# Masked attention on one core: how finished tokens are turned back and added to x, and which engine squares the queries

## The chip, the core and the metric

The kernel runs on one core of one Trainium2 chip. The core has TensorE (PE, matrix multiplies; its weight loads are shown apart as PEld), VectorE (DVE), ScalarE (ACT), GpSimd (POOL) and SyncE (SP), which only starts transfers (DMAs) here. Each engine works through its own queue in order. The metric is the time of one execution in microseconds (us), as the median of several runs.

## The reference

x has 8 batches of 512 features and 1,024 tokens, and the mask has one 0 or 1 for each token of a batch. There are 8 heads of 64 features; queries, keys and values are the same projection.

```python
xt = jnp.transpose(x, (0, 2, 1))
q = xt @ Wq.T
qh = q.reshape(B, T, NH, dk).transpose(0, 2, 1, 3)
scores = scale * jnp.einsum('bhqd,bhkd->bhqk', qh, qh)
logits = (scores * cmask + (1.0 - cmask) * NEG) * rmask
attn = jax.nn.softmax(logits, axis=-1)
ctx = jnp.einsum('bhqk,bhkd->bhqd', attn, qh)
out = ctx.transpose(0, 2, 1, 3).reshape(B, T, D) @ Wo.T
return x + jnp.transpose(out, (0, 2, 1))
```

A masked token attends evenly to all tokens, so every masked token of a batch has the same result, and no token attends to a masked key except those.

## The kernel before

About half of the tokens of a batch are kept by the mask. The kernel gathers them (at most 575, in 5 chunks of 128, the last of 64), puts the mean of x in the last place for all masked tokens, runs attention on these 576 tokens alone, and spreads the results back over the 1,024 tokens. (A second function, `attention_of_all_tokens`, does the same without gathering, and runs only where a mask keeps too many tokens or a sum gets too small; it doesn't run here.)

The work is a sequence of 32 pairs (b, pr): batch b from 0 to 7 and, in each, pr from 0 to 3, two heads of 64 features at a time. The document calls the stretch of a pair a stage. The order of all instructions is written by hand: the loop in `late` (L1067) goes through the pairs, and in each through five chunks c of keys. In a chunk stand `scores` (TensorE: 8 matmuls into `s`; ScalarE: two exps into `e`, L616), `add_up` of the chunk before (VectorE: the sums of `e`, L633), and tasks for other pairs that `tasks_of` (L884) lists with a cost and that are spread over the chunks by these costs; at the end of the pair comes `attend` (L657: TensorE, 40 matmuls into `av`, copied to `cT` by ScalarE). `s` has two buffers.

What the steps touch:

- Queries: `project` (L534) for the pair two places ahead, then `values` (L554): TensorE turns the queries into `v`, ScalarE copies it out (L565), VectorE squares it (`sq`, L570), sums the squares (`len`, L572) and takes the maximum (`top`, L579). `bias_of` (L581) turns `top` into the exps' bias, a pair later.
- End of a pair: `add_up(before, LAST)` and `invert(before)` (L713) in chunk 0 of the next pair: VectorE makes inverses `ri`, turns them (`rt`, L719), SP stores them and loads them back as `rb`. `contexts(before)` (L742) multiplies `cT` by `rb` on VectorE, in chunk 2, 3, 3 or 4 for pr = 0, 1, 2, 3.
- Next x: `turn` (L430), four times a batch, in pr=0 chunks 0, 2, 4 and pr=1 chunk 1: VectorE turns 128x1024 elements in 32x32 blocks (`xt`, L444), writing the four features of a row side by side, and SP stores `xt` to DRAM (`xd`, L452), four transfers of 32 rows. `search` (VectorE) finds which rows are kept, and `gather` (GpSimd, `xin`, L507) fetches them at the end of pr=1. `collect` (L515) turns `xin` into `xc` on TensorE at the beginning of pr=2.
- Output of batch b-1: `output` (L752) in pr=0 (two chunks), pr=1 (two) and pr=2 (one): TensorE multiplies the four `cT` of the batch by Wo into `po`, the fourth of them the `cT` of the pair just before, when the batch has just begun. ScalarE copies `po` to `oc`, GpSimd stores it to DRAM (`od`).
- Back to all tokens: `load_rest` (L809) loads x of batch b-1 again in pr=1 chunk 2 (`xr`, eight tiles of 128x512). `fetch` (L830) in pr=3 gathers, for each of eight groups of 128 tokens, the rows of `od` that these tokens own (`g`, L833; `origin` says which). `finish` (L841), eight tasks in pr=3: TensorE turns four 128x128 squares of `g` into `o` (L845), VectorE adds `o` from PSUM to `xr` (L848), and SP stores `xr` to the output (L850). `issue_stores` (L876) sends a store one chunk after its task.
- The last two batches end otherwise: batch 6 is finished by `finish` after the last pair, batch 7 by `finish_tokens`.

The tiles that pass through PSUM take turns in four banks (`bank`), besides the four that `s` takes.

Of the kernel before, what the change touches and what calls it, by code (L numbers as in the profile page):

```python
# [21 lines left out]
Q = 32  # L22
# [296 lines left out]
def attention_of_kept_tokens(ctx, tc, x, mask, wq, wo, out, ident, wqT, woT, verdict, flag):  # L319
# [49 lines left out]
    key = keep.tile([P, NC], F32, name="key")  # L369
    kept = keep.tile([P, B], F32, name="kept")  # L370
    origin = keep.tile([P, B, NT], I32, name="origin")
    pads = keep.tile([P, B, NC], F32, name="pads")
    pens = keep.tile([P, B, NC], F32, name="pens")
    low = keep.tile([P, 2, LAST], F32, name="low")
# [179 lines left out]
    def values(pair):  # L554
        nm = "%d_%d" % pair
        qT = qTs[pair]
        v = sb.tile([P, NC, P], F32, tag="v", name=f"v_{nm}", bufs=4)
        for at, n in ((0, LAST), (LAST, 1)):
            pt = bank(f"v_{nm}_{at}")
            for i in range(n):  # L560
                c = at + i
                nc.tensor.transpose(  # L562
                    pt[:, i * P : (i + 1) * P], qT[:, c * P : (c + 1) * P], ident
                )
            nc.scalar.copy(  # L565
                v[:, at : at + n, :], pt[:, : n * P].rearrange("p (c d) -> p c d", d=P)
            )
        vs[pair] = v
        sq = sb.tile([P, NC, P], F32, tag="sq", name=f"sq_{nm}", bufs=1)
        nc.vector.tensor_tensor(sq, v, v, ALU.mult)  # L570
        lengths = sb.tile([P, 2 * NC], F32, tag="len", name=f"len_{nm}")
        nc.vector.tensor_reduce(  # L572
            lengths,
            sq.rearrange("p c (h d) -> p (c h) d", h=2),
            axis=AX.X,
            op=ALU.add,
        )
        tops[pair] = sb.tile([P, 1], F32, tag="top", name=f"top_{nm}")
        nc.vector.tensor_reduce(tops[pair], lengths, axis=AX.X, op=ALU.max)  # L579
# [213 lines left out]
    def end_output(b, i):  # L793
# [12 lines left out]
        nc.vector.tensor_tensor(oc[:n, :], po[:n, :], partials[i][:n, :], ALU.add)  # L806
        nc.sync.dma_start(ods[b][places[i], :], oc[:n, :])

    def load_rest(b):  # L809
        for r in range(NN):  # L810
            for d in range(ND):
                xr = sb.tile([P, NB], F32, tag="xr", name=f"xr_{b}_{r}_{d}", bufs=NN * ND)
                nc.sync.dma_start(xr, x[b, d * P : (d + 1) * P, r * NB : (r + 1) * NB])
                xrs[b, r, d] = xr

    def fetch_last(b):

# [12 lines left out]
    def fetch(b):  # L830
        for i in range(NT):
            g = sb.tile([P, D], F32, tag="g", name=f"g_{b}_{i}", bufs=NT)
            nc.gpsimd.indirect_dma_start(  # L833
                out=g,
                out_offset=None,
                in_=ods[b],
                in_offset=bass.IndirectOffsetOnAxis(ap=origin[:, b, i : i + 1], axis=0),
            )
            gs[b, i] = g

# [43 lines left out]
    def tasks_of(p):  # L884

        b, pr = pairs[p]
        front, back, end = [], [], []
        if p + 2 < len(pairs):
            ahead = pairs[p + 2]
            front = [(2.0, lambda hf=hf: project(ahead, hf)) for hf in range(2)]  # L890
            front.append((0.6, lambda: values(ahead)))
            if p == 0:
                behind = pairs[1]
                front = [
                    (2.0, lambda: project(behind, 1)),
                    (0.6, lambda: values(behind)),
                    front[0],
                    (0.3, lambda: bias_of(behind)),
                    *front[1:],
                ]  # L900
        if p == ND - 1:
            back = [(0.5, lambda d=d: turn_weights(woT, "wo", d)) for d in range(ND)]
        if b + 1 < B and pr == 2:
            front = [(0.5, lambda i=i: collect(b + 1, i)) for i in range(NC)] + front
        if b > 0:
            if pr < 3:
                mine = {0: (0, 1), 1: (2, 3), 2: (4,)}[pr]
                (back if pr else end).extend((3.6, lambda i=i: output(b - 1, i)) for i in mine)
            elif b + 1 < B:
                t = 0.5  # L910
                back += [(t, lambda r=r, d=d: finish(b - 1, r, d)) for r in range(NN) for d in range(ND)]
        if p + 1 == len(pairs):
            end = [(2.7, lambda i=i: begin_output(b, i)) for i in range(NC)]
        return mix(front, back) + end
# [29 lines left out]
    def early():  # L944
# [98 lines left out]
        mean_first()  # L1043
        pt = bank("home_t")
        nc.tensor.transpose(pt[:, :BC], home, ident[:BC, :BC])
        nc.vector.tensor_copy(origin, pt[:, :BC].rearrange("p (b c) -> p b c", c=NT))

    def late():
        weights["wq"] = load_weights(wq, "wq")
# [14 lines left out]
        bias_of(pairs[0])  # L1064

        TURN = [(0, 0), (0, 2), (0, 4), (1, 1)]
        for p, pair in enumerate(pairs):  # L1067
            b, pr = pair
            before = pairs[p - 1] if p else None
# [3 lines left out]
            for c in range(NC):  # L1073
                scores(pair, c)
                if c:
                    add_up(pair, c - 1)
                if c == 0 and before:
                    add_up(before, LAST)
                    if p + 1 < len(pairs):
                        invert(before)  # L1080
                    else:
                        inv = inverses(before)
                if p + 1 == len(pairs):
                    if c == 1:
                        spread(before, inv)
                        contexts(before)
                elif c == (2, 3, 3, 4)[pr] and before:
                    contexts(before)
                if 0 < p < len(pairs) - 1 and c == 1:
                    bias_of(pairs[p + 1])  # L1090
                if b + 1 < B:
                    if (pr, c) in TURN:
                        turn(b + 1, TURN.index((pr, c)))
                    if pr < 2 and pr * NC + c < NN * ND:
                        add_features(b + 1, pr * NC + c)
                    if pr == 1 and c == LAST:
                        mean_of(b + 1)
                    if pr == 1:
                        search(b + 1, c)
                    if pr == 0 and c == 1:  # L1100
                        queries_of(b + 1)
                    if pr == 1 and c == LAST:
                        for i in range(NC):
                            gather(b + 1, i)
                if pr == 2 and c == 0 and b + 2 < B:
                    load_batch(b + 2)
                    load_ranks(b + 2)
                if pr == 1 and c == 2 and b > 0:
                    load_rest(b - 1)
                if pr == 3 and c == 0 and b > 0:  # L1110
                    fetch(b - 1)
                while todo and (c or p + 1 < len(pairs)) and (done < share * (c + 1) - 0.3 or c == LAST):
                    cost, task = todo.pop(0)
                    task()
                    done += cost
                issue_stores()
# [125 lines left out]
```

## Time and profile before

| what | value |
|---|---|
| median of 3 runs | 776.83 us (776.33 to 778.43) |
| the profiled execution | 778.43 us, of which its span from first to last instruction is 776.2 us |
| mean granted TensorE clock over the span | 0.966 |
| TensorE busy | 710.6 us |
| VectorE busy | 546.8 us |
| ScalarE busy | 356.6 us |
| DMA traffic | 119.53 MB, 154 GB/s |
| one batch in the middle (four stages) | some 90 us |

A busy time is the time in which an engine had an instruction in work, over the whole span. A wait in the profile names the instruction that stood, what released it, the total, the number of times and the longest. A group of instructions has its line, engine, operation, tiles and shapes, its count, the busy time, the mean duration of one in nanoseconds, and the idle time of the engine just before them. A timeline row has its start and its duration; rows of VectorE may overlap by some 0.08 us, so that steps from start to start are a little shorter than durations. In a row of windows stand the stretch, its length, the busy time of PE, PEld, DVE, ACT and POOL, the granted clock, the share of DMA time and the GB/s.

### The profile page before, as it was taken

To read this page: it belongs to the slowest core of one execution; us is meant where nothing else is said; L and a number is where in the kernel's file an instruction comes from. 1 tells how busy PE (TensorE), PEld (TensorE's weight loads), DVE (VectorE), ACT (ScalarE), POOL (GpSimd) and SP (SyncE) were. 2 spreads that over 40 slices of the span, in tenths; PEclk is the share of its full clock that TensorE was granted. 3 is DMA by queue.
4 is the path that set the end of the run, shared out by engine and by line. 5 is a ranking of instruction groups with operands and counts; after the bars stand their busy time and mean duration, and the time that the engine had idled before them with its cause. 6 is when DMAs were issued, how large, how long until landed. Compare 5 with 4: busy or idle time off the path is not lost.

```text
span 776.2 us, 12232 instructions
## 1 busy us (share of the span) xinstructions
PE 710.6 (92%) x4187; PEld 407.8 (53%) x4187; DVE 546.8 (70%) x1517; ACT 356.6 (46%) x727; POOL 168.9 (22%) x208
## 2 busy tenths in 40 slices
PE   6699898999989998999989999899989999898984
PEld 5555564556544564446635565445645566454443
DVE  6189878676867778586976768777785867556353
ACT  3366465454534544545444545345454444345300
POOL 4712010043102510034100521025100340004021
PEclk9799999999989999999989999999999999999996
DMA  7543503477235752377243773367532742146138
GB/s 272 164 144 112 175 19 91 119 239 258 99 93 164 217 217 79 106 212 268 100 128 105 221 253 127 99 193 222 177 107 79 226 136 90 64 153 204 38 126 266
DMA packets 86713, 119.53 MB, mean 154 GB/s; under 512 B 15744, under 2 KB 48576, under 8 KB 86640
## 3 DMA queue, kind: packets, MB, share of 16 engines
q1 hardware_dynamic: 69888, 76.27, 31.5%
q0 software_dynamic: 12528, 40.28, 15.9%
q10 hardware_dynamic: 4224, 2.10, 0.9%
q8 instruction: 35, 0.57, 0.3%
q14 instruction: 38, 0.31, 0.1%
HBM read 75.41 MB, written 43.19 MB: 153 GB/s over the span
## 4 chain that ended last, share of the span: by engine, by line
PE 69%; DVE 11%; DMA 6%; ACT 5%; issue 4%; SPq 1%; POOL 1%; POOLq 0%; DVEq 0%; ACTq 0%
PE s L612 17%; PE av L649 16%; PE pq L543 15%; PE po L762 10%; DMA xin<-xd,source 4%; ACT e L616 3%; PE o L845 3%; PE xc L522 3%; DVE junk L633 2%; DVE xt L444 2%; PE pa L782 2%; PE v L562 1%; ACT v L565 1%; DVE len L572 1%; DMA xr<-in_x_dram 1%
## 5 line engine op out<-in xcount | busy, mean ns | idle before, releaser
L633 DVE CUSTOM_DVE_ANT_0 junk<-e,valid 128x576 f32<-128x576 f32 x256 | 193.4, 756 | 77.9 <-ACT e L616 73.1
L612 PE MATMUL s<-qT 64*128 64x288 f32 (+1 forms) x1280 | 190.3, 442 | 7.8 <-ACT e L616 6.9
L616 ACT ACTIVATE e<-s,bias 128x576 f32<-128x576 f32 x256 | 176.6, 742 | 33.9 <-PE s L612 27.3
L612 PEld LDWEIGHTS s<-qT 64*128 64x128 f32 (+1 forms) x1280 | 95.1, 179 | 98.0 <-issue 57.5
L762 PE MATMUL po<-woT,cT 128*128 128x512 f32 (+1 forms) x336 | 124.4, 551 | 20.2 <-DVE cT L745 20.2
L543 PE MATMUL pq<-xc,wqT 128*128 128x288 f32 x512 | 138.1, 415 | 0.0
L649 PE MATMUL av<-e,v 128*64 128x288 f32 x1024 | 132.4, 409 | 0.9 <-DVE m L587 0.2
L543 PEld LDWEIGHTS pq<-xc,wqT 128*128 128x128 f32 x512 | 92.7, 190 | 36.3 <-issue 9.6
L649 PEld LDWEIGHTS av<-e,v 128*64 128x64 f32 x1024 | 71.1, 137 | 53.5 <-issue 7.0
L771 POOL DMA_DIRECT2D od<-oc x42 | 23.9, 570 | 331.1 <-ACT oc L769 312.4
L762 PEld LDWEIGHTS po<-woT,cT 128*128 128x128 f32 (+1 forms) x336 | 49.3, 178 | 78.4 <-issue 48.3
L665 ACT COPY cT<-av 128x288 f32<-128x288 f32 x62 | 22.4, 401 | 143.5 <-PE av L649 86.7
L833 POOL DMA_INDIRECT g<-od,origin x56 | 61.0, 1089 | 38.9 <-issue 17.2
L769 ACT COPY oc<-po 128x512 f32<-128x512 f32 (+1 forms) x35 | 19.1, 547 | 97.0 <-PE po L762 97.0
L444 DVE STREAM_TRANSPOSE xt<-x 128x1024 f32<-128x1024 f32 x28 | 57.7, 2062 | 0.0
L550 ACT COPY qT<-pq 128x288 f32<-128x288 f32 x64 | 25.5, 399 | 65.8 <-PE pq L543 61.5
L507 POOL DMA_INDIRECT xin<-xd,source x40 | 40.4, 1010 | 48.0 <-DVE sums L633 30.4
L570 DVE TENSOR_TENSOR sq<-v 128x640 f32<-128x640 f32 x32 | 26.3, 820 | 27.3 <-ACT v L565 22.8
L495 DVE TENSOR_SCALAR_CACHE_REDUCE junk<-rank,key 128x1024 f32<-128x1024 f32 (+4 forms) x40 | 39.9, 998 | 1.0 <-ACT rank L1015 0.8
L848 DVE TENSOR_TENSOR xr<-o,xr 128x512 f32<-128x512 f32 x56 | 36.3, 683 | 5.2 <-PE o L845 3.4
L587 DVE TENSOR_REDUCE m<-top 128x1 f32<-128x128 f32 x32 | 9.3, 289 | 41.2 <-PE top L585 41.0
L633 DVE CUSTOM_DVE_ANT_0 junk<-el,part 128x288 f32<-128x288 f32 x64 | 29.1, 454 | 12.1 <-ACT el L616 10.9
(133 smaller groups left out, 656.3 us busy)
## 6 DMA issues: line engine op xcount, KB each, us to landing
xr<-in_x_dram SPq DMA_DIRECT2D x64, 256.0 KB
x<-in_x_dram SPq DMA_DIRECT2D x56, 256.0 KB
xd<-xt SPq DMA_DIRECT2D x112, 128.0 KB
out_dram<-xr SPq DMA_DIRECT2D x56, 256.0 KB
rb<-row SPq DMA_DIRECT2D x60, 160.0 KB
od<-oc POOLq DMA_DIRECT2D x28, 256.0 KB
rank<-ranks SPq DMA_DIRECT2D x6, 512.0 KB
xd<-xt POOLq DMA_DIRECT2D x8, 256.0 KB
```

The lines of the kernel that those rows point to most:

```text
L444: nc.vector.transpose(xt.rearrange("p k (f d) -> p k d f", d=ND), xs[b][r][:, :, at : at + n].rearrange("p d (k t) -> p k d t", t=Q),)
L495: nc.vector.tensor_scalar(junk[:, :n], rank[:, i * P :], key[:, col], 0.0, ALU.is_le, ALU.add, accum_out=found[:, col])
L507: nc.gpsimd.indirect_dma_start(out=xin[:n, :], out_offset=None, in_=xds[b], in_offset=bass.IndirectOffsetOnAxis(ap=searches[b][2][:n, i : ...
L543: nc.tensor.matmul(pq[:, :KH], wqT[:, d, pr * P : (pr + 1) * P], xcs[b][:, d, cols], start=(d == 0), stop=(d == ND - 1),)
L570: nc.vector.tensor_tensor(sq, v, v, ALU.mult)
L612: nc.tensor.matmul(s[to, h, :KH], qT[heads[h], keys], qT[heads[h], queries], start=True, stop=True)
L616: nc.scalar.activation(e[:, hf if c < LAST else 0, :, :], s[:, :, :KH], AF.Exp, bias=biases[pair][:, c : c + 1], scale=SCALE,)
L633: nc.vector.tensor_tensor_reduce(junk[:, :n].rearrange("p (f k) -> p f k", k=KH), e[:, :, h, :], (valid if c < LAST else part).rearrange(" ...
L649: nc.tensor.matmul(av[head, :KH], v[keys, c, head], e[keys, hf if c < LAST else 0, h, :], start=(c == 0), stop=(c == LAST),)
L762: nc.tensor.matmul(po[k * n : (k + 1) * n, :w], cTs[b, pr][:, i * P : i * P + n], woT[:, pr, k * w : (k + 1) * w], start=(pr == 0), stop=( ...
L833: nc.gpsimd.indirect_dma_start(out=g, out_offset=None, in_=ods[b], in_offset=bass.IndirectOffsetOnAxis(ap=origin[:, b, i : i + 1], axis=0),)
L848: nc.vector.tensor_tensor(xr, pt, xr, ALU.add)
```

## The change

For batches 0 to 5 (`BLOCKS`), TensorE's transposes of `finish` are replaced by VectorE's 32x32 blocks. `block_origin` deals the tokens to `g` in another order, so that after a transpose of each 32x32 block the partitions hold 32 features and a quarter of the tokens: quadrant a (32 partitions) holds tokens 256 a to 256 a + 255, features on its 32 partitions and in 16 steps along the row. `place_blocks` makes `block_origin` by 16 small copies in pair (0, 2). `finish_blocks` turns one `g` into `o` (128x512) and adds it to its part of `xr`, which is one tile of 16 x 256 elements per partition in one buffer. x is loaded to it, and the result stored from it, by four transfers each, one per quadrant, with 32 partitions as the outer dimension and pieces of 256 tokens (1 KB). The eight blocks of a batch are no tasks any more: `FINISH` puts two each in chunks 2, 3 and 4 of pr=3, after `contexts` in chunk 4, and one each in chunks 0 and 1 of the next pr=0; the four stores follow in chunk 2. Batches 6 and 7 end as before, except that batch 6's `xr` tiles are parts of one tile.

The squares in `values` move from VectorE to ScalarE, in all 32 pairs.

```diff
--- before.py
+++ after.py
@@ -369,6 +369,8 @@
     key = keep.tile([P, NC], F32, name="key")
     kept = keep.tile([P, B], F32, name="kept")
     origin = keep.tile([P, B, NT], I32, name="origin")
+    placed = keep.tile([P, B, NT], F32, name="placed")
+    block_origin = keep.tile([P, B, NT], I32, name="block_origin")
     pads = keep.tile([P, B, NC], F32, name="pads")
     pens = keep.tile([P, B, NC], F32, name="pens")
     low = keep.tile([P, 2, LAST], F32, name="low")
@@ -567,7 +569,7 @@
             )
         vs[pair] = v
         sq = sb.tile([P, NC, P], F32, tag="sq", name=f"sq_{nm}", bufs=1)
-        nc.vector.tensor_tensor(sq, v, v, ALU.mult)
+        nc.scalar.activation(sq, v, AF.Square)
         lengths = sb.tile([P, 2 * NC], F32, tag="len", name=f"len_{nm}")
         nc.vector.tensor_reduce(
             lengths,
@@ -806,12 +808,47 @@
         nc.vector.tensor_tensor(oc[:n, :], po[:n, :], partials[i][:n, :], ALU.add)
         nc.sync.dma_start(ods[b][places[i], :], oc[:n, :])
 
+    BLOCKS = range(B - 2)
+
+    def place_blocks():
+
+        for a in range(A):
+            for j in range(A):
+                nc.vector.tensor_copy(
+                    block_origin[a * Q : (a + 1) * Q, :, j::A],
+                    placed[j * Q : (j + 1) * Q, :, a * (NT // A) : (a + 1) * (NT // A)],
+                )
+
+    def in_blocks(t):
+        return t.rearrange("(k f) (a n) -> a f k n", f=Q, a=A)
+
     def load_rest(b):
+        xr = sb.tile([P, D // Q, T // A], F32, tag="xr", name=f"xr_{b}", bufs=1)
+        if b in BLOCKS:
+            for a in range(A):
+                nc.sync.dma_start(xr[a * Q : (a + 1) * Q, :, :], in_blocks(x[b])[a])
+            xrs[b] = xr
+            return
+        xr = xr.rearrange("p k n -> p (k n)")
         for r in range(NN):
             for d in range(ND):
-                xr = sb.tile([P, NB], F32, tag="xr", name=f"xr_{b}_{r}_{d}", bufs=NN * ND)
-                nc.sync.dma_start(xr, x[b, d * P : (d + 1) * P, r * NB : (r + 1) * NB])
-                xrs[b, r, d] = xr
+                part = xr[:, (r * ND + d) * NB : (r * ND + d + 1) * NB]
+                nc.sync.dma_start(part, x[b, d * P : (d + 1) * P, r * NB : (r + 1) * NB])
+                xrs[b, r, d] = part
+
+    def finish_blocks(b, i):
+        o = sb.tile([P, D // Q, Q], F32, tag="o", name=f"o_{b}_{i}", bufs=2)
+        nc.vector.transpose(o.rearrange("p k t -> p (k t)"), gs[b, i])
+        xr = xrs[b]
+        to = xr[:, :, i * Q : (i + 1) * Q]
+        nc.vector.tensor_tensor(to, o, to, ALU.add)
+        if i == NT - 1:
+
+            def store():
+                for a in range(A):
+                    nc.sync.dma_start(in_blocks(out[b])[a], xr[a * Q : (a + 1) * Q, :, :])
+
+            stores[0].append(store)
 
     def fetch_last(b):
 
@@ -834,7 +871,9 @@
                 out=g,
                 out_offset=None,
                 in_=ods[b],
-                in_offset=bass.IndirectOffsetOnAxis(ap=origin[:, b, i : i + 1], axis=0),
+                in_offset=bass.IndirectOffsetOnAxis(
+                    ap=(block_origin if b in BLOCKS else origin)[:, b, i : i + 1], axis=0
+                ),
             )
             gs[b, i] = g
 
@@ -906,9 +945,6 @@
             if pr < 3:
                 mine = {0: (0, 1), 1: (2, 3), 2: (4,)}[pr]
                 (back if pr else end).extend((3.6, lambda i=i: output(b - 1, i)) for i in mine)
-            elif b + 1 < B:
-                t = 0.5
-                back += [(t, lambda r=r, d=d: finish(b - 1, r, d)) for r in range(NN) for d in range(ND)]
         if p + 1 == len(pairs):
             end = [(2.7, lambda i=i: begin_output(b, i)) for i in range(NC)]
         return mix(front, back) + end
@@ -1043,7 +1079,8 @@
         mean_first()
         pt = bank("home_t")
         nc.tensor.transpose(pt[:, :BC], home, ident[:BC, :BC])
-        nc.vector.tensor_copy(origin, pt[:, :BC].rearrange("p (b c) -> p b c", c=NT))
+        nc.vector.tensor_copy(placed, pt[:, :BC].rearrange("p (b c) -> p b c", c=NT))
+        nc.vector.tensor_copy(origin, placed)
 
     def late():
         weights["wq"] = load_weights(wq, "wq")
@@ -1064,6 +1101,14 @@
         bias_of(pairs[0])
 
         TURN = [(0, 0), (0, 2), (0, 4), (1, 1)]
+
+        FINISH = {
+            (ND - 1, 2): (0, 1),
+            (ND - 1, 3): (2, 3),
+            (ND - 1, 4): (4, 5),
+            (0, 0): (6,),
+            (0, 1): (7,),
+        }
         for p, pair in enumerate(pairs):
             b, pr = pair
             before = pairs[p - 1] if p else None
@@ -1109,6 +1154,12 @@
                     load_rest(b - 1)
                 if pr == 3 and c == 0 and b > 0:
                     fetch(b - 1)
+                if p == 2 and c == 2:
+                    place_blocks()
+                for i in FINISH.get((pr, c), ()):
+                    of = b - 1 if pr == ND - 1 else b - 2
+                    if of in BLOCKS and of >= 0:
+                        finish_blocks(of, i)
                 while todo and (c or p + 1 < len(pairs)) and (done < share * (c + 1) - 0.3 or c == LAST):
                     cost, task = todo.pop(0)
                     task()
```

## The prediction

> **What bounds the kernel now.** I read the busy shares first, then the waits, then the stages of one batch, then the timeline around the longest TensorE wait. The page's first row:
>
> ```profile
> PE 710.6 (92%) x4187; PEld 407.8 (53%) x4187; DVE 546.8 (70%) x1517; ACT 356.6 (46%) x727; POOL 168.9 (22%) x208
> ```
>
> TensorE seems to be the bound and VectorE to have 30% to spare. An average hides stages, so next the waits (engine, line, releaser: total us, times, longest), and the stages of batch 4 (stage, length; busy time of PE, PEld, DVE, ACT, POOL; granted clock; DMA share; GB/s). The first three rows are pr=3 of batch 4, pr=0 and pr=1 of batch 5; the last is the 6.8 us after TensorE's wait:
>
> ```profile
> PE po L762 <- DVE cT L745: 20.2, 7, 3.0
> DVE sq L570 <- ACT v L565: 22.8, 13, 5.0
> ```
>
> ```profile
> 364.80:382.80 18.00, 17.87 (x130) 11.71 (x130) 15.07 (x36) 8.50 (x18) 1.80 (x1) 1.00 0.34 124
> 382.80:411.00 28.20, 25.25 (x122) 12.77 (x120) 21.79 (x57) 12.67 (x29) 2.08 (x4) 0.88 0.37 106
> 411.00:435.70 24.70, 24.52 (x136) 13.01 (x134) 17.67 (x50) 11.47 (x25) 6.12 (x7) 1.00 0.56 176
> 396.50:403.30 6.80, 6.76 (x14) 2.90 (x15) 5.04 (x11) 2.67 (x5) 0.65 (x1) 0.55 0.41 116
> ```
>
> One wait matters: seven times, 2.9 us each, TensorE stands in pr=0 before the fourth matmul of the first `po`, until VectorE has finished `cT` of the pair before (`contexts`, chunk 2). After it the clock is 0.55. This is where VectorE is full: 15.1 + 21.8 = 36.9 us in the 46.2 us of pr=3 and pr=0. The timeline (start, duration) shows the only long pause in VectorE's queue and the end of the wait:
>
> ```profile
> 391.12 0.83 DVE L570 TENSOR_TENSOR sq<-v 128x640 f32<-128x640 f32 x1 [1.24 <-ACT v L565]
> 395.73 0.76 DVE L745 TENSOR_TENSOR cT<-cT,rb 128x576 f32<-128x576 f32 x1
> 396.54 2.08 PE L762 MATMUL po<-woT,cT 128*128 128x512 f32 x2 [2.95 <-DVE cT L745]
> ```
>
> The change puts work into exactly this stretch of this queue. Prices (count | busy, mean ns):
>
> ```profile
> L444 DVE STREAM_TRANSPOSE xt<-x 128x1024 f32<-128x1024 f32 x28 | 57.7, 2062 | 0.0
> L848 DVE TENSOR_TENSOR xr<-o,xr 128x512 f32<-128x512 f32 x56 | 36.3, 683 | 5.2 <-PE o L845 3.4 <-remote 1.8
> L845 PE MATMUL o<-ident,g 128*128 128x128 f32 x224 | 30.9, 278 | 0.0
> L570 DVE TENSOR_TENSOR sq<-v 128x640 f32<-128x640 f32 x32 | 26.3, 820 | 27.3 <-ACT v L565 22.8 <-issue 2.9 <-ACT el L616 1.6
> L719 DVE STREAM_TRANSPOSE rt<-ris 128x32 f32<-128x32 f32 x30 | 6.4, 212 | 1.0
> L461 ACT ACTIVATE junka<-x 128x512 f32<-128x512 f32 x56 | 35.4, 632 | 0.0
> ```
>
> **Removed from TensorE.** Batches 0 to 5 lose 32 transposes each in pr=3: 32 x 0.138 us (30.9/224) = 4.4 us. Without them TensorE meets ScalarE's exps in chunks 2 and 4 (two `s` buffers, 1.37 us for a chunk's two exps), and I give back 1.0: pr=3 ends 3.4 us earlier, and TensorE is at the `po` at 390.2 instead of 393.6. That pays only if `cT` is there.
>
> **Added to VectorE: a block.** One transpose of 128x512 and one add of two SBUF tensors, eight a batch: six in pr=3, two in pr=0, all ahead of `contexts`. The add: L848 has as many elements; three in a row start 0.61 us apart. The transpose has no row of its size. Above: half of L444, 1.03 us. Below: L848's 0.68, 512 elements of a dense operation. Nearest is L719, the same operation dense on both sides (211 to 214 ns every time), while L444 writes its elements 16 bytes apart and wanders from 1,994 to 2,133 ns. So 212 ns plus 480 elements at 1.04 ns (0.97 by L570 and L745: 820 - 758 for 64 elements) = 0.71. Dependent operations here start 0.03 after the end: a block is 0.71 + 0.03 + 0.61 = 1.35 us; ends 1.29 and 1.67.
>
> L444 costs 2.01 ns an element. [...]
>
> **Squares to ScalarE.** VectorE loses 0.85 us at each `values`. ScalarE pays 0.68 (L565's copies, 582 ns for 512 and 279 for 128, extended) to 0.79 (L461 x 640/512); I take 0.73. In pr=1 to 3 it lies under the attend matmuls (ScalarE's `cT` copy waits 4.7 us for them), in pr=0 under the `po` wait (5.7 us idle): nothing. Without cover: 32 x 0.73 = 23 us.
>
> **The walk from pr=3 of batch 4 to `cT`.** VectorE's queue, by start-to-start steps of the timeline. Its start: the exps of chunk 1 end at 368.87 in both kernels; today three adds stand ahead, after the change the sums of chunk 1 start at 368.92. Then, without a pause: five pairs of sums of `e` at 1.48 = 7.5; eight blocks 10.8; `contexts` of pr=3 2.2; two length and maximum steps 1.9; last sums and inverses 2.3; one x transpose 1.9; `bias` 0.7; `contexts` to `cT` 2.1. That is 29.3 us, so `cT` is there at 398.2, today 396.5: **1.7 us later**. Check by differences: eight blocks for five later adds (+10.8 - 3.0), squares -1.7, shorter `contexts` -0.3, pauses at `sq`, `m` and the adds gone -2.3, earlier start -1.7: +1.8. TensorE waits 8.0 us instead of 2.9. Everything behind it (one `po`, two score chunks, the second `po`, attend) moves by 1.7, and VectorE is idle again in chunk 3 (1.7 us today), so each batch pays anew. It happens in pr=0 of batches 2 to 6: 5 x 1.7 = 8.5; in batch 7, without an x transpose, VectorE has 1.9 less: `cT` 0.5 later. **+9.0 us.**
>
> **The clock.** After the wait, clocks of 0.55, 0.75, 0.55, 0.75, 0.76 over 6.8 us in batches 2 to 6 cost 3.1 + 1.7 + 3.1 + 1.7 + 1.6 = 11.2 us; batches 1 and 7 none. With 8 us of idling I expect all six between 0.5 and 0.75, 2.55 us each: 15.3. **+4.1** (bounds -1 to +9).
>
> **Queues and DMAs.** Eight loads and eight stores of 128 rows become four and four of 32 rows, 1 KB pieces. SP issues 8 fewer (0.48 us each); the stores, now behind block 7, go out at pr=0 chunk 2, where the DMA share is 0.37; behind them stand the `xd` stores of the next x, not needed before the gather 30 us later. The load waits for these stores (one `xr` buffer): some 25 us apart, enough for 2 MB. But the load takes 424.5 to 432.5 at a DMA share of 0.91, and the gather of `xin` (issued 429.3) sends its first packets at 432, for TensorE at 434.5; TensorE already waits for it (`xc` for `xin`, 15.1 us in six waits, the longest 10.0). A longer load goes on the path. Median packets: 84 ns for 2 KB here, 27 ns for the 512 bytes of the 32-row `xd` stores; 46 for 1 KB (+0.8 us a load) to 54 (+2.3); part is swallowed. I take 0.35 x 6 = **+2**; bounds 0 and 14.
>
> [...] No row has a load into 32 rows.
>
> The 16 small copies of `place_blocks` (0.15 us each, like L746) stand in pr=2 of batch 0, where VectorE's queue is idle in the next stage (11.6 of 17.4 us): nothing, or 2.4 uncovered. The extra copy at the start: +0.2.
>
> **Sum.** 9.0 + 4.1 + 2 + 0.2 = 15.3 on the span of 776.2 gives 791.5; the profiled run is 2.2 longer (778.4), so 793.7; the median, 776.8, is 1.6 below that run: **792 us**.
>
> **Rivals.** (1) The transpose costs what L444 does: 1.67 a block, 8 x 0.32 = 2.6 more a batch, 6 x 2.6 = 15: 807. For it: the only large row of this operation. Against it: its scattered writes. (2) The 32-row loads delay the gather by the full 2.3 us: +12 over my 2: 804. For it the 0.91; against it that the `xd` stores from 32 rows show no slow packets. (3) Faster: VectorE's queue absorbs the blocks and TensorE's 3.4 us come through, 6 x 3.4 = 20: 756 at most. It decides at a block step of 1.35 - 1.7/8 = 1.14 us, a transpose of 0.50; each 0.1 below buys 4.8 us; I put it at 766. For it: 30% idle on the page and L570's 26 us gone. Against it: 512 elements in 0.50 us is below one per 1.04 ns. (4) No change: small errors of the walk (0.2 us a block) cancel the 1.7 and the clock is no worse: 777.
>
> **Chances.** Forecast 0.62; rivals 0.11, 0.09, 0.12, 0.06. Within 0.3% is 774.5 to 779.2, about what a measurement here can tell from no change. Slower 0.82, same 0.06, faster 0.12. The forecast's own range is 784 to 800; with the slower rivals taken in and half of the rest left out, 779 to 808.
>
> **What would show it.** Right: an `o` transpose near 0.71 us, VectorE without a pause from pr=3 chunk 1 to `cT`, a `po` wait of 8 us in batches 2 to 6, 49 us over all, clocks near 0.6 behind each. Wrong: `po` waits no longer than 2.9 us, a block under 1.14 us, or `xc` waiting for `xin` by more than 2 us a batch.

## The result, and the profile after

The changed kernel takes 817.77 us (median of 4 runs, 814.78 to 823.45); the kernel before took 777.63 us (776.33 to 779.98) beside it. The ratio is 1.0521, with an interval of 1.0458 to 1.0585: 5% slower. The forecast was 792 us, with 808 us as the upper end. So the sign was right and the size was not. The profiled execution of the changed kernel is the run of 823.45 us (span 821.7; before 776.2), so 45.5 us of span have to be found.

The busy shares of the changed kernel, for the row that opened the prediction:

```profile
PE 707.9 (86%) x3995; PEld 393.8 (48%) x3995; DVE 556.7 (68%) x1550; ACT 381.7 (46%) x759; POOL 165.6 (20%) x208
```

TensorE has 192 instructions fewer and is busy 2.7 us less, but its share falls from 92% to 86%: it waits more. The waits of the changed kernel and, last, the one of the kernel before that belongs to the second (engine, line, releaser: total us, times, longest):

```profile
PE po L764 <- DVE cT L747: 48.3, 7, 8.4
...
PE xc L524 <- DMA xin<-xd,source: 31.1, 8, 9.4
```

```profile
PE xc L522 <- DMA xin<-xd,source: 15.1, 6, 10.0
```

The first is the wait that the prediction was about (20.2 before, 49 foretold). The second was 15.1 us before, and is the one that was priced too low. (Batch 4's wait, 3.36 us, is not in it: the profile puts it down to ScalarE's exps, which ended at that moment. In the kernel before the same `xc` starts ahead of these exps, 434.54 against 436.49, so they do not hold it.) A count by stages separates the two. It takes the time from a pair's first `scores` matmul to that of the next pair; batches are counted from 0 (the stretch that the prediction calls pr=3 of batch 4 and pr=0 of batch 5 is batch 3 and batch 4 so counted).

| us | pr=0 before, after | pr=1 | pr=2 before, after | pr=3 before, after |
|---|---|---|---|---|
| batch 1 | 25.4, 26.8 | 22.6, 22.6 | 21.1, 25.3 | 19.0, 16.0 |
| batch 2 | 28.3, 33.6 | 22.6, 22.6 | 21.4, 28.0 | 19.0, 16.0 |
| batch 3 | 27.0, 32.8 | 22.6, 22.6 | 21.0, 26.4 | 19.0, 16.0 |
| batch 4 | 28.2, 33.5 | 22.6, 22.6 | 20.7, 26.1 | 19.0, 16.0 |
| batch 5 | 27.0, 32.2 | 22.6, 22.6 | 21.0, 25.8 | 19.1, 16.4 |
| batch 6 | 26.9, 33.4 | 22.6, 22.6 | 20.9, 26.0 | 19.0, 16.0 |
| batch 7 | 25.0, 30.7 | 22.7, 22.6 | no gather | |
| all, after less before | +35.2 | 0 | **+31.5** | -17.9 |

The rest is -3.2 us, in batch 0, the start and the end. Two costs stand side by side: pr=3 and pr=0 together cost 17.3 us, and pr=2 costs 31.5. The timeline of the changed kernel (start, duration; in brackets the wait ahead) shows one of each; the middle row is TensorE's first `xc` of batch 3, the last that of `cT` in batch 4:

```profile
357.37 1.24 PE L614 MATMUL s<-qT 64*128 64x288 f32 x8
362.89 1.09 PE L524 MATMUL xc<-ident,xin 128*128 128x128 f32 x4 [4.29 <-DMA xin<-xd,source]
...
418.87 2.08 PE L764 MATMUL po<-woT,cT 128*128 128x512 f32 x2 [7.94 <-DVE cT L747]
```

In the kernel before, the same `xc` matmuls:

```profile
344.30 0.63 PE L522 MATMUL xc<-ident,xin 128*128 128x128 f32 x4 [0.70 <-DMA xin<-xd,source]
```

Not only is the wait 4.29 us instead of 0.70: behind it the same four matmuls take 1.09 us instead of 0.63. The windows give the cause (stretch, length; PE, PEld, DVE, ACT, POOL; granted clock; DMA share; GB/s). Of the changed kernel, the 2 MB load of `xr` in batch 4, the 6.8 us behind the wait for `xin`, and the 6.8 us behind the wait for `cT`:

```profile
447.00:458.40 11.40, 10.03 (x68) 4.79 (x66) 10.61 (x37) 3.64 (x8) 5.42 (x6) 1.00 1.05 206
460.40:467.20 6.80, 6.76 (x30) 3.68 (x31) 1.53 (x5) 1.76 (x4) 1.14 (x2) 0.56 0.36 95
418.90:425.70 6.80, 6.80 (x14) 2.91 (x15) 5.07 (x11) 2.67 (x5) 0.65 (x1) 0.52 0.90 200
```

Of the kernel before, the same load and the stretch behind the same `xc`:

```profile
424.50:432.50 8.00, 8.00 (x52) 3.90 (x50) 7.66 (x24) 2.03 (x5) 3.15 (x4) 1.00 0.91 284
434.40:441.20 6.80, 6.10 (x44) 3.40 (x43) 4.96 (x21) 4.88 (x9) 2.21 (x3) 1.00 0.56 115
```

In these windows the load takes 11.4 us instead of 8.0: 206 GB/s at a DMA share of 1.05 where 284 went through at 0.91. The transfer engines are full and move less. From its first packet to its last the load takes 11.9 us in batch 4 and 12.8 to 15.6 in the other five, against 8.0 to 8.5 before; the last packets run beside those of the gather. Behind the longer load the clock is 0.56 where it was 1.00; in the same stretch of batches 1 to 6 it is 0.75, 0.60, 0.67, 0.56, 0.75 and 0.62, and before 1.00 in all six.

The gather stands behind this load. SyncE and GpSimd in the changed kernel:

```profile
446.13 2.13 SPq L829 DMA_DIRECT2D xr<-in_x_dram  x4
```

```profile
450.75 0.54 POOL L773 DMA_DIRECT2D od<-oc  x1 [9.31 <-ACT oc L771]
451.85 1.04 POOL L509 DMA_INDIRECT xin<-xd,source  x1 [0.56 <-DVE cT L748]
```

The records of single packets show none on GpSimd's queue from 448 to 457.45. The store of `oc` ahead of the gather was issued at 450.75, the gather at 451.85, so both stand some 6 us, until the load is nearly through. In experiment 12, with no load there, the same queue's packets start 1.1 us after the issue of that store. Counted from the start of pr=1, they start at 24.3 to 24.5 us in batches 1 to 6 here, and at 20.7 to 21.6 in the kernel before: 3.2 us later on average. The packets of the load, medians of 128 in turn, take 46 ns for the first 128 to 384, then mostly 80 to 98 ns for 1 KB; the kernel before has 84 ns for 2 KB.

The priced instructions, from the groups of the changed kernel (count | busy, mean ns):

```profile
L841 DVE STREAM_TRANSPOSE o<-g 128x512 f32<-128x512 f32 x48 | 33.8, 704 | 0.0
L844 DVE TENSOR_TENSOR xr<-o,xr 128x512 f32<-128x512 f32 x48 | 33.2, 693 | 1.6
...
L572 ACT ACTIVATE sq<-v 128x640 f32<-128x640 f32 x32 | 23.6, 737 | 1.0
```

They are what was assumed: 0.71, 0.68 and 0.73 us. From the 128x32 transpose (212 ns) to this one, each of the 480 elements more costs 1.03 ns; the prediction took 1.04.

### The profile page after: what moved, and what is told of

Its sections match the earlier page's. It is cut to its first block, busy times and chain, and to the rows that moved or that the text cites. A ratio compares the mean times of both kernels' runs of the same rounds, so it can differ in the third digit from the quotient of the medians.

```text
span 821.7 us, 11761 instructions
## 1 busy us (share of the span) xinstructions
PE 707.9 (86%) x3995; PEld 393.8 (48%) x3995; DVE 556.7 (68%) x1550; ACT 381.7 (46%) x759; POOL 165.6 (20%) x208
## 4 chain that ended last, share of the span: by engine, by line
PE 52%; DVE 25%; DMA 9%; issue 7%; ACT 4%; POOL 1%; SPq 0%; another core or an unknown queue 0%; POOLq 0%; DVEq 0%; ACTq 0%
PE s L614 12%; PE po L764 12%; PE av L651 11%; PE pq L545 9%; DMA xin<-xd,source 6%; DVE junk L635 6%; DVE o L841 3%; DVE xr L844 3%; ACT e L618 3%; DVE xt L446 2%; PE xc L524 2%; DVE junk L497 2%; DVE cT L747 2%; PE pa L784 1%; DVE len L574 1%
## 5 line engine op out<-in xcount | busy, mean ns | idle before, releaser
L614 PE MATMUL s<-qT 64*128 64x288 f32 (+1 forms) x1280 | 193.7, 447 | 6.7 <-ACT e L618 4.7
L764 PE MATMUL po<-woT,cT 128*128 128x512 f32 (+1 forms) x336 | 139.3, 637 | 48.3 <-DVE cT L747 48.3
L614 PEld LDWEIGHTS s<-qT 64*128 64x128 f32 (+1 forms) x1280 | 96.9, 182 | 103.5 <-issue 61.9
L545 PEld LDWEIGHTS pq<-xc,wqT 128*128 128x128 f32 x512 | 92.7, 190 | 38.6 <-issue 11.2
L764 PEld LDWEIGHTS po<-woT,cT 128*128 128x128 f32 (+1 forms) x336 | 54.9, 208 | 113.7 <-issue 58.0
L667 ACT COPY cT<-av 128x288 f32<-128x288 f32 x62 | 22.3, 401 | 110.2 <-PE av L651 82.2
L446 DVE STREAM_TRANSPOSE xt<-x 128x1024 f32<-128x1024 f32 x28 | 57.6, 2059 | 0.4 <-DMA rank<-ranks 0.4
L870 POOL DMA_INDIRECT g<-od,block_origin x48 | 50.2, 1046 | 34.6 <-issue 30.3
L524 PE MATMUL xc<-ident,xin 128*128 128x128 f32 (+1 forms) x160 | 24.5, 296 | 34.5 <-DMA xin<-xd,source 31.1
L509 POOL DMA_INDIRECT xin<-xd,source x40 | 39.4, 984 | 45.7 <-DVE sums L635 28.3
L574 DVE TENSOR_REDUCE len<-sq 128x10 f32<-128x640 f32 x32 | 26.0, 813 | 33.3 <-ACT sq L572 22.6
L635 DVE CUSTOM_DVE_ANT_0 junk<-el,part 128x288 f32<-128x288 f32 x64 | 29.1, 454 | 15.2 <-ACT el L618 13.9
```

Of the source, the lines that this page charges most:

```text
L446: nc.vector.transpose(xt.rearrange("p k (f d) -> p k d f", d=ND), xs[b][r][:, :, at : at + n].rearrange("p d (k t) -> p k d t", t=Q),)
L509: nc.gpsimd.indirect_dma_start(out=xin[:n, :], out_offset=None, in_=xds[b], in_offset=bass.IndirectOffsetOnAxis(ap=searches[b][2][:n, i : ...
L524: nc.tensor.transpose(pt[:, d * n : (d + 1) * n], xin[:n, d * P : (d + 1) * P], ident[:n, :n])
L545: nc.tensor.matmul(pq[:, :KH], wqT[:, d, pr * P : (pr + 1) * P], xcs[b][:, d, cols], start=(d == 0), stop=(d == ND - 1),)
L574: nc.vector.tensor_reduce(lengths, sq.rearrange("p c (h d) -> p (c h) d", h=2), axis=AX.X, op=ALU.add,)
L614: nc.tensor.matmul(s[to, h, :KH], qT[heads[h], keys], qT[heads[h], queries], start=True, stop=True)
```

## The experiments

The theory after the result: two causes, separate from each other: VectorE's blocks ahead of `cT` (pr=0), and the load into 32 rows, which holds up the gather (pr=2). Rivals: that one of them makes the other; that the squares cost; that the short pieces, not the 32 rows, are slow. Stage lengths below are those of batches 1 to 6 unless another is named. Every ratio is to runs of the kernel before on the same chip, whose median is given because it differs from chip to chip and from one set of runs to the next.

**1. The changed kernel with its load at pr=1 chunk 0, two chunks sooner.**

```diff
-                if pr == 1 and c == 2 and b > 0:
+                if pr == 1 and c == (0 if b - 1 in BLOCKS else 2) and b > 0:
                     load_rest(b - 1)
```

> The changed kernel, with its load of x by quadrants moved from chunk 2 to chunk 0 of pr=1 (batches 0 to 5). Theory: most of the loss is the load running into the gather of xin. Stage pr=2 (from the first scores matmul of one pair to that of the next) took 20.7 to 21.4 us before and 25.3 to 28.0 after in batches 1 to 6, 31.5 us in all; with the load out of the way TensorE's waits for xin (3.4 to 4.3 us each) and the low clock behind them go: some 786 us against 818. Rival 1: the loss is VectorE's queue alone: no change, 818. Rival 2: the gather itself has become slower: pr=2 stays above 24 us.

787.27 us (before 778.89), ratio 1.0113 [1.0044, 1.0182]. pr=2 goes back to 19.9 to 22.0 us, pr=0 stays at 31.8 to 33.1 in batches 2 to 6. Its waits:

```profile
PE po L764 <- DVE cT L747: 47.8, 7, 8.3
...
PE xc L524 <- DMA xin<-xd,source: 15.6, 6, 9.0
```

The wait for `xin` is back at its old size and the one for `cT` is untouched. Where the load stands is worth some 30 us.

**2. The changed kernel without the block transposes.**

```diff
-        o = sb.tile([P, D // Q, Q], F32, tag="o", name=f"o_{b}_{i}", bufs=2)
-        nc.vector.transpose(o.rearrange("p k t -> p (k t)"), gs[b, i])
+        o = gs[b, i].rearrange("p (k t) -> p k t", t=Q)
```

> The changed kernel without the 48 block transposes of finish_blocks: g is added to xr as it is, so tokens and features land in the wrong places. Everything else, the loads and stores too, stays. Theory: the transposes (0.70 us each) are what makes cT late; without them 8 x 0.7 = 5.6 us leave VectorE's queue in pr=3 and pr=0, the wait for cT falls from about 8 us to about 3, and pr=0 from 33 us to 28: 6 x 5 = 30 us less, some 788. Rival: the loss is the transfers' alone: 818, waits for cT unchanged.

779.05 us, ratio 0.999 [0.9959, 1.0021], 9 us less than expected. pr=0 is 25.2 to 26.9, pr=2 stays at 25.2 to 26.7. The waits are the mirror image of the first experiment:

```profile
PE xc L524 <- DMA xin<-xd,source: 35.1, 9, 10.0
...
PE po L764 <- DVE cT L747: 18.9, 7, 2.8
```

So neither cause makes the other.

**3. The changed kernel with the squares on VectorE again**, and **4. the kernel before with the squares alone on ScalarE.**

```diff
-        nc.scalar.activation(sq, v, AF.Square)
+        nc.vector.tensor_tensor(sq, v, v, ALU.mult)
```

> The changed kernel with the squares back on VectorE. Theory: two squares (0.85 us each) stand again in the queue between chunk 1 of pr=3 and cT, so cT is 1.7 us later in six batches: +10 us, some 828. Rival: ScalarE's square costs something on the path itself, and taking it back gains: 816 or less.

828.08 us, ratio 1.0608 [1.0535, 1.0681]. The wait for `cT` grows by 9.1 us:

```profile
PE po L764 <- DVE cT L747: 57.4, 7, 9.8
```

```diff
-        nc.vector.tensor_tensor(sq, v, v, ALU.mult)
+        nc.scalar.activation(sq, v, AF.Square)
```

> The kernel before with the squares on ScalarE, nothing else changed. Theory: cT waits there for v and not for VectorE's load, and 0.74 us on ScalarE replace 0.85 on VectorE in the same chain: -0.1 us a batch, 776 to 777. Rival: VectorE's relief is worth more, 1.7 us a batch: 766. Rival 2: the square delays ScalarE's next exps: 780 or more.

776.5 us (before 778.89), ratio 0.9967 [0.9925, 1.0009]: the interval holds 1. Moving the squares is worth these 9.1 us of waiting where VectorE's queue sets `cT` (the ratios of the changed kernel with and without it, 1.0521 and 1.0608, differ by some 7 us, and their intervals overlap), and nothing measurable where it does not. It is not a cause of the loss.

**5. The kernel before with its load in eight transfers of 32 rows, pieces of 2 KB**, and **6. in eight of 128 rows, pieces of 1 KB.** Only the shape of the transfers differs; `finish` reads the same elements.

```diff
+        whole = sb.tile([P, ND, NN, NB], F32, tag="xr", name=f"xr_{b}", bufs=1)
+        rows = x[b].rearrange("(d a f) (r n) -> a f d r n", a=A, f=Q, r=NN)
+        for a in range(A):
+            for r in range(NN):
+                nc.sync.dma_start(whole[a * Q : (a + 1) * Q, :, r, :], rows[a, :, :, r, :])
...
```

> The kernel before, in which only load_rest is changed: eight transfers of 32 rows (one quadrant each), pieces of 2 KB, in the place of eight of 128 rows with pieces of 2 KB; the tiles hold the same data and nothing else changes. Theory A: 32 rows make the load slow (2 MB in some 11 us instead of 8). Then the gather comes 3 us later, TensorE waits 3 to 4 us for xin in each of seven batches and runs on a low clock behind it: stage pr=2 goes from 21 to some 26 us, 30 us in all, some 806. Theory B: the 1 KB pieces make it slow; here they are 2 KB, so no change, 777.

796.54 us (before 781.53), ratio 1.0233 [1.0149, 1.0316]. pr=2 is 22.8 to 26.3 us, packets of 2 KB take some 170 ns instead of 84, and the wait for `xin` nearly doubles:

```profile
PE xc L522 <- DMA xin<-xd,source: 28.6, 9, 9.3
```

```diff
...
+        rows = x[b].rearrange("(d p) t -> p d t", p=P)
+        for j in range(2):
+            for k in range(4):
+                at = slice(k * 256, (k + 1) * 256)
+                nc.sync.dma_start(whole[:, 2 * j : 2 * j + 2, at], rows[:, 2 * j : 2 * j + 2, at])
...
```

> The kernel before, in which only load_rest is changed: eight transfers of 128 rows with pieces of 1 KB in the place of 2 KB. Theory A (32 rows make the load slow): a 1 KB piece takes some 46 ns, the load 0.8 us longer, pr=2 some 1 us longer: 777 to 784. Theory B (1 KB pieces make it slow): the load takes 11 us, some 806.

779.08 us, ratio 0.9991 [0.9953, 1.0028]; 1 KB packets take 46 ns, pr=2 is 20.8 to 21.6 us but for one of 24.2. The 32 rows are slow, the short pieces are not. The 46 ns of the prediction was the right figure for the wrong shape. Neither run reaches the whole loss: over batches 1 to 6, pr=2 is 21.4 us longer than in the kernel before in experiment 5 (theory A had 30 in all) and 3.5 us in experiment 6, where the changed kernel has 31.5. The 32 rows by themselves thus show two thirds of it; 32 rows and 1 KB together were not run in the kernel before.

**7. The changed kernel with its blocks spread behind `cT`** (pr=0 chunks 3 and 4, pr=1 chunks 0 and 4, pr=2 chunks 0 to 3) **and the load in pr=3 chunk 1**, behind the stores of the one `xr` buffer.

```diff
-            (ND - 1, 2): (0, 1),
...
-            (0, 1): (7,),
+            (0, 3): (0,),
+            (0, 4): (1,),
+            (1, 0): (2,),
+            (1, 4): (3,),
...
+            (2, 3): (7,),
...
-                if pr == 1 and c == 2 and b > 0:
+                if pr == 3 and c == 1 and b > 0:
                     load_rest(b - 1)
```

> The changed kernel with both causes taken away and nothing left out: the eight blocks stand behind contexts of the next pr=0 (chunks 3 and 4), in pr=1 (chunks 0 and 4) and in pr=2 (chunks 0 to 3), and x is loaded by quadrants in pr=3 chunk 1, far from the gather of xin. Theory: VectorE isn't full before cT any more, so the 3.1 us that pr=3 has lost stay gained, the wait for cT is 2.8 us as before, and pr=2 is near 20 us because no load stands before the gather: about 4 us a batch below before, some 753. Rival: the blocks in pr=1 and pr=2 delay VectorE's work for the gather or the bias there, and the gain is given back: 770 or more.

776.94 us (before 781.53), ratio 0.9962 [0.9923, 1.0001]. The 753 was missed: pr=2 is 20.7 and pr=3 16.0, but pr=0 of batches 3 to 6 is 31.3 to 34.7 (26.7 in batch 2, 27.7 in batch 7). VectorE's waits name a new releaser; the second view is VectorE's timeline, the third SyncE's, of the same stretch:

```profile
DVE rb L739 <- DMA rb<-row: 43.1, 10, 7.4
```

```profile
374.30 0.22 DVE L739 TENSOR_TENSOR rb<-rb 128x64 f32<-128x64 f32 x1 [4.99 <-DMA rb<-row]
```

```profile
352.89 4.58 SPq L849 DMA_DIRECT2D out_dram<-xr  x4
357.57 9.58 SPq L724 DMA_DIRECT2D row<-rt  x4
368.87 1.09 SPq L729 DMA_DIRECT2D rb<-row  x2
370.76 3.04 SPq L829 DMA_DIRECT2D xr<-in_x_dram  x4
```

The stores go at the end of pr=2. The small `row` transfers of the next `invert` need 9.58 us behind them (some 1.4 us elsewhere), `rb` is issued late, and VectorE stands in `contexts` for it; then the load is in the way of the next `rb`. The 2 MB were moved from the path of `xin` to the path of `rb`.

**8. The kernel before with its own load at pr=1 chunk 0.**

```diff
-                if pr == 1 and c == 2 and b > 0:
+                if pr == 1 and c == 0 and b > 0:
                     load_rest(b - 1)
```

> The kernel before with load_rest two chunks earlier (chunk 0 of pr=1 instead of chunk 2). Theory: in the kernel before, the load already ends just when the gather's first packets go out, so TensorE's short waits for xin (0 to 1.5 us a batch) go: 1 us a batch, 770 to 775. Rival: the gather isn't held up by a load of 128 rows: no change, 777.

777.32 us (before 781.53), ratio 0.9955 [0.9921, 0.999], a smaller gain than expected. pr=2 is 20.6 to 20.7 throughout. Little of the kernel before was lost in this place.

**9. Experiment 7 with two `xr` buffers.** The load then need not follow the stores: it goes to pr=1 chunk 0, and the stores to pr=3 chunk 1, behind `rb`. Room comes from fewer buffers for `v`, `el`, `rb` and `oc`, and from putting `o` into a scratch tile.

```diff
-        xr = sb.tile([P, D // Q, T // A], F32, tag="xr", name=f"xr_{b}", bufs=1)
+        xr = sb.tile([P, D // Q, T // A], F32, tag="xr", name=f"xr_{b}", bufs=2)
...
-            stores[0].append(store)
+            late_stores.append(store)
...
-                if pr == 3 and c == 1 and b > 0:
+                if pr == 1 and c == 0 and b > 0:
                     load_rest(b - 1)
+                if pr == 3 and c == 1 and late_stores:
+                    late_stores.pop()()
```

> The kernel with the blocks late, but with two buffers for xr, so that the load need not follow the stores: the load goes to pr=1 chunk 0 and the four stores to pr=3 chunk 1, behind the transfers of rb. To make room, o lies in the sums' scratch tile, and v, el, rb and oc have fewer buffers. Theory (in the kernel with the blocks late, rb came late behind 2 MB of stores and then of load, VectorE stood at sum_last for it, 43.1 us in ten waits, and cT with it): rb is no longer late, pr=0 of batches 3 to 6 is 26.7 to 27.7 us as in batches 2 and 7 there, where it was 31.3 to 34.7, 24 us less in all; the early load costs pr=2 up to 1 us a batch: 750 to 760 us, and VectorE's waits for rb under 15 us. Rival (the blocks themselves, or ScalarE's squares, hold VectorE's queue in pr=0): cT stays as late, 770 us or more.

759.79 us (before 780.75), ratio 0.9751 [0.9709, 0.9793]: faster than both kernels. pr=0 of batches 3 to 6 is 25.2 to 26.8, and the wait for `cT` 19.0 us in all; VectorE's waits name no `rb` transfer any more. pr=2 is 20.2 to 20.5 in batches 2, 3 and 6, and 22.1 to 22.3 in the others.

**10. The changed kernel with quadrants 2 and 3 of the load on ScalarE's queue.**

```diff
-                nc.sync.dma_start(xr[a * Q : (a + 1) * Q, :, :], in_blocks(x[b])[a])
+                queue = nc.sync if a < 2 else nc.scalar
+                queue.dma_start(xr[a * Q : (a + 1) * Q, :, :], in_blocks(x[b])[a])
```

> The changed kernel with one edit: quadrants 2 and 3 of the load of xr are issued on ScalarE's DMA queue instead of SyncE's, so that they can run beside quadrants 0 and 1. [...] Theory B (a packet into 32 rows is slow by itself, or two queues share what there is): the load ends when it did, pr=2 stays at 25.8 us or more, 810 to 820 us.

841.14 us (before 780.75), ratio 1.0791 [1.0731, 1.0852]. That lies above the 810 to 820 us of theory B, and it does not decide whether a second queue helps, because the two halves never ran together. By the profile, SyncE's `row` transfers came to stand behind ScalarE's half; the changed kernel has 0.4 us of this wait, the kernel before none:

```profile
SPq L724 <- DMA xr<-in_x_dram: 84.6, 5, 18.3
```

In batches 2 to 6 SyncE's half is issued 11 to 12 us behind the other, at the end of pr=1, and the gather waits for that. Why `row` waits for this load is open. From first packet to last, ScalarE's half, 1 MB, took 5.5 to 6.8 us, and SyncE's 6.4 to 8.0.

**11. The kernel before with its load cut by partitions in another way in each batch.**

```diff
...
+        cuts = ((0, 128), (0, 32, 64, 96, 128), (0, 64, 128), (0, 32, 96, 128))[b % 4]
+        for lo, hi in zip(cuts, cuts[1:]):
+            for r in range(NN):
+                nc.sync.dma_start(whole[lo:hi, :, r, :], rows[lo:hi, :, r, :])
...
```

> The kernel before, with its load of x for the sum (2 MB, 2 KB pieces, at the same place) cut by partitions in another way in each batch: batches 0 and 4 in transfers of all 128 rows, batches 1 and 5 of 32, batches 2 and 6 of 64 (0 to 63, then 64 to 127), batch 3 of rows 0 to 31, 32 to 95 and 96 to 127. Measured are the packets and the length of each load. [...] Theory B (fewer rows are slower in proportion, or the number of transfers decides): 64 rows lie halfway, 120 ns or less and 9 to 10 us, and rows 32 to 95 are like any 64.

Five windows, each the length of one load (batches 0 to 4: 128 rows; 32; 64; 32, 64 and 32; 128):

```profile
153.80:160.50 6.70, 6.70 (x45) 3.28 (x45) 6.39 (x19) 1.97 (x4) 2.47 (x3) 1.00 1.03 349
242.30:254.00 11.70, 9.63 (x67) 4.58 (x65) 11.12 (x39) 4.04 (x8) 5.65 (x6) 1.00 1.03 232
334.50:345.70 11.20, 9.39 (x67) 4.50 (x65) 10.61 (x38) 4.04 (x8) 5.66 (x6) 1.00 1.02 212
427.60:435.70 8.10, 8.10 (x59) 3.81 (x57) 7.75 (x25) 1.97 (x4) 3.56 (x4) 1.00 1.04 279
517.90:524.60 6.70, 6.70 (x44) 3.29 (x44) 6.39 (x19) 1.97 (x4) 2.35 (x3) 1.00 1.02 340
```

A transfer of 64 rows is as slow as one of 32 (11.2 and 11.7 us, against 6.7 for 128). In batch 3 the packets, medians of 128 in turn, take some 84 to 88 ns in the middle transfer, rows 32 to 95, and some 170 in the outer ones: that load needs 8.1 us. So in these loads neither the number of rows nor that of transfers decides, but which rows go together; why they do was not shown. pr=2 behind these loads, in the same order: 19.9, 23.3, 26.1, 20.5, 19.9 us. Theory B fails: it had 9 to 10 us for 64 rows, and rows 32 to 95 like any 64. The whole took 779.73 us (before 770.18).

**12. Experiment 9 with the load at pr=0 chunk 3.**

```diff
-                if pr == 1 and c == 0 and b > 0:
+                if pr == 0 and c == 3 and b > 0:
                     load_rest(b - 1)
```

> The kernel with two xr buffers, with its load four chunks earlier, at pr=0 chunk 3. There the load stands ahead of the last xd stores of the next x on SyncE's queue, so that they, and the gather behind them, go 2 to 3 us later (issued 20 us into pr=1, 18.7 in the kernel before), and pr=2 is 22.1 to 22.3 us in batches 1, 4 and 5 but 20.2 to 20.5 in the others. Theory (that is the load still in the gather's way): pr=2 is 20.5 in all batches, 5 us less, 753 to 757 us. Rival (the load now delays rb of pr=1 or the xd stores as much): 759 us or more.

753.84 us (751.27 to 755.58; before 770.18), ratio 0.9788 [0.9759, 0.9817]. pr=2 is 19.9 to 20.2 us in all batches, as the theory said; the ratio does not tell it from experiment 9 (the intervals overlap, and the kernel before took 770.18 us beside it). Its busy row and waits:

```profile
PE 688.0 (92%) x3995; PEld 385.2 (51%) x3995; DVE 559.9 (75%) x1550; ACT 380.2 (51%) x759; POOL 171.7 (23%) x208
```

```profile
PE po L764 <- DVE cT L747: 19.0, 7, 2.8
...
PE xc L524 <- DMA xin<-xd,source: 12.3, 4, 10.2
```

With both causes out of the way, the change gains: 2.5% in experiment 9 and 2.1% in 12, some 16 to 19 us of the 26.5 that 192 transposes of 0.138 us take. TensorE's share is 92% again, over a span of 749.7 us. The first two experiments take 0.041 and 0.053 off the changed kernel's ratio, together 0.094; experiments 9 and 12, with neither cause but with all the work done, take off 0.077 and 0.073. Part of the difference may be the work that experiment 2 leaves out; it was not measured apart.

## Why the prediction was right in sign and wrong in size

**The failed step is the load.** "46 for 1 KB (+0.8 us a load) to 54 (+2.3); part is swallowed. I take 0.35 x 6 = +2; bounds 0 and 14." It measured 31.5 us. A sign of being wrong that the prediction had named, `xc` waiting for `xin` by more than 2 us a batch, is what came: 3.4 to 4.3 us in all six. There are three errors:

- The price. The packet was priced between rows that are not of its kind: the load of 2 KB pieces goes into 128 rows, and the 32-row `xd` transfers, 27 ns for 512 bytes, are stores. Loads into 32 rows have mostly 80 to 98 ns for 1 KB and some 170 for 2 KB, about twice what 128 rows have. The load became 3.9 us longer in batch 4 and more in the others, above the upper bound of 2.3.
- The swallowing. Counted from the start of pr=1, the first `xc` begins on average at 27.7 us instead of 24.4 (batches 1 to 6). These 3.25 us a batch, 19.5 in all, are the 3.2 by which the packets of the gather's queue start later: nothing is swallowed. TensorE had nothing to spare there: before, it was already idle for 0.1 to 1.5 us ahead of this `xc`. (That slight idling is what the prediction should have read: of its 15.1 us of waits for `xin`, 12.2 lie in batch 0 and ahead of it, where this load does not run, and 2.9 here.)
- The consequence that was left out. The remaining 12.0 us lie behind the wait: six stretches of 6.8 us at the clocks above, where it was 1.00, lose 13.9 us of full-speed time. The prediction reckoned with exactly this behind the wait for `cT` and forgot it behind the wait for `xin`.

What should have widened the range stood in the prediction: no row has a load into 32 rows, and its bounds rest on other rows all the same. The measured load took 11.9 us in batch 4 and more in the others. Experiment 11 has loads of 64 rows, 0 to 63 and 64 to 127, as slow as those of 32 (11.2 and 11.7 us), and packets into rows 32 to 95 as short as those into 128 (84 to 88 ns); what makes the difference was not shown. Rival 2 had the right mechanism, the loads that delay the gather, and, at 804 us, the same price error.

**VectorE's walk was right, somewhat short.** From the start of pr=3 to the `cT` that the `po` waits for, the changed kernel needs 2.2, 1.8, 1.9, 1.9 and 2.8 us more in batches 2 to 6 (1.7 foretold), 0.4 less in batch 7 (0.5 more foretold) and 0.2 less in batch 1: together +10.0 for the +9.0. pr=3 is 3.05 us shorter (3.4 foretold; 2.7 in batch 5), the wait 7.94 us in batch 4 (8.0 foretold), 48.3 in all (49 foretold). Experiment 2 shows the blocks as the cause: without their transposes the wait is 18.9 us. The price of the transpose came near (0.704 us for 0.71), but its 1.04 ns an element was the author's estimate, which names no row; the run shows 1.03, and the 0.97 from L570 and L745 would have made 0.68 us.

**The clock behind `cT` was mis-sized**: +7.2 us for +4.1, 17.3 less the 10.0 of the walk. The clocks over the 6.8 us behind the seven waits are 0.75, 0.53, 0.60, 0.52, 0.70, 0.60 and 0.55; as the prediction reckons they cost 18.7 us where it had 15.3 (11.2 before). It had them in batches 2 to 7; batch 1, whose wait stayed at 2.8 us, got 1.7 us of it too.

**The squares** cost ScalarE 0.737 us and nothing on the path (experiment 4), and VectorE's relief by them is worth what the walk gave it: experiment 3 puts 9.1 us on the waits, 1.3 to 1.6 in each of six batches, where two squares of 0.85 had been reckoned. **`place_blocks`** and the start cost nothing that shows: batch 0 and the start are shorter by 2.4 us. (The shortest `xt` transpose is 1,990 ns, not the 1,994 of the prediction; nothing rests on it.)

Put right in its one step, the sum is 793.7 - 2 + 31.5 = 823.2 us for the profiled run, which took 823.45. That it comes out so near is luck: the walk and the clock came out 4.1 higher, and small gains at the start and the end, which nobody had foretold, offset them.

## What to carry to other kernels

Price a transfer by a row with the same direction and the same partitions, not only the same piece; where none is there, the bound has to be wide: here loads into 32 rows have mostly 80 to 98 ns for 1 KB where 128 rows have 46. Ask of each large transfer which small, urgent one stands behind it: here 2 MB that take 3.9 us longer or more cost 31 us in six batches in front of a gather, 2 MB of stores and of load in front of `rb` cost some 28 us (pr=0 of batches 3 to 6 in experiments 7 and 9), and in a place with neither (experiment 12) nothing shows. A new wait of TensorE costs its own length and, behind every wait of 3.3 us or more in the profiles of the two kernels, a lower clock over the next 6.8 us (0.50 to 0.75); both belong in the sum, at every place where it waits.

## What the runs showed of the hardware that was not expected

- 2 MB of 2 KB pieces into 128 rows take 6.4 to 6.7 us in two transfers (experiment 11), and 10.7 to 11.7 us in transfers of 32 rows or of rows 0 to 63 and 64 to 127; a transfer into rows 32 to 95 has packets as short as one into 128 (84 to 88 ns for 2 KB against some 170).
- A VectorE transpose in 32x32 blocks of 128x512 f32 takes 704 ns when it writes densely. The one of 128x1024 that writes four bytes in every 16 takes 2,059; half of that, for 512 elements, would be 1,030.
- Behind waits of 3.4 to 4.3 us for `xin` the granted clock is 0.56 to 0.75 over 6.8 us; behind the shorter waits of before (0.70 us in batch 3) it stays at 1.00. Between them it is not settled: behind 2.9 us for `cT` it is 0.55 to 1.00 in the kernel before.
- GpSimd's queue, with a store and the gather issued at 450.75 and 451.85, sent no packet before 457.45, when a load on SyncE's queue was nearly through; without that load (experiment 12) its packets started 1.1 us after the issue. A queue of its own did not bring the gather past the load.
